# Attention over a graph in one kernel: wider k and q loads by broadcast, two chunks of adj in one load, and a rebuilt head

## Chip, core and metric

The kernel runs on one core of a Trainium2 chip. Its time is the device time of one execution in microseconds (us), given as the median of several runs. One more execution was profiled; the views shown below come from it.

## What is computed

Two layers over a graph of 2708 nodes with 128 features each. Layer 0 is attention with the adjacency matrix added twice to the scores; layer 1 is a two-hop graph convolution. Each adds its input and normalises. Cut to what matters:

```python
# layer 0: x (2708, 128), adj (2708, 2708), 8 values per query ("heads" are the inner dimension)
q = (x @ Wq.T).reshape(128, 2708, 8)        # a reshape of the flat product, not a transpose
k = (x @ Wk.T).reshape(128, 2708, 8)
v = (x @ Wv.T).reshape(128, 2708, 8)
a = einsum('dnh,dmh->dnm', q, k) * 128 ** -0.5 + adj + adj
out = einsum('dnm,dmh->dnh', softmax(a, axis=2), v).reshape(2708, 1024)
x = layernorm(x + out @ Wo.T)
# layer 1
hidden = adj @ (x @ W2) + b2
x = layernorm(x + adj @ (hidden @ W4) + b4 + hidden @ res_w.T + res_b)
```

So 128 separate attentions over 2708 x 2708 scores are to be made, each with an inner dimension of 8. Because q, k and v are reshapes of the flat product, attention d reads rows d x 2708 / 128 and on of the projection: the first four attentions need the first 85 of the 2708 rows of x, and no more.

## The kernel before

**Stages.** There are three. The head projects the first 256 rows of x and loads the first keys. The attention stage runs over 32 groups of GB = 4 attentions, in each over 6 blocks of QB = 452 queries, in each over 9 steps: 1728 steps. The end divides by the sums, applies Wo, and computes layer 1. All engines run an order written out at build time (manual_schedule): each engine's queue holds its instructions in program order, so an instruction that waits holds up all behind it on that engine. Nearly all loads and stores stand on SP's queue.

**A step.** Keys are cut into 22 chunks m: 21 of 128 and a short one of 20 (number NU = 21). Scores of two (chunk, attention) pairs at a time go to PSUM (`score`, L451), DVE adds the adj tile (`add_near`, L458) and writes them to e, ACT takes the exponential of up to eight of them at once (L559). For nine chunks (TWO_EXP) the exponentials of scores and of adj are taken apart: ACT L556 makes w from scores in PSUM, and POOL L557 multiplies w by the exponential of adj (ecol), which is computed once in group 0, stored in DRAM (ne), and loaded in all later groups. PE then adds the products with the values (`add_up`, L468 to L476), and `hand_on` (L479) copies the sums to SBUF and stores them (os). `interleave` fixes the order of PE's work from a table of costs.

**Loads.** `load_adj` (L303) loads one tile of [128, 452] of adj, stored with chunk rows contiguous (adjP): `col` tiles of one chunk, `two` tiles of two chunks (two loads; the short chunk comes from adjS), or an `ecol`. The loop keeps 8 such loads ahead of the step it is at. `load_keys` (L261) brings k of the next group to SBUF (k_raw): 128 partitions, of which 8 at a time get the high or low half of the split k, in 16 loads. Each half stands in two places, since a score is a product of sums: k high and low against q high and low. The loads stand in steps 0, 2, 4 to 30 of the group before. `order_keys` then puts k in order of chunks (9 casts on POOL, L275), `load_values` and `spread_values` do the same for v. `load_q` (L295) loads q of the next block (8 loads of 16 rows, at step 3 of a block).

**Projections.** `project_all` (head) makes 128 rows of K, Q or V at once, splits K and Q into a high and a low part (ACT L402, DVE L403), and returns the store. The rest of the rows are projected by quarters inside the attention loop (`load_quarter`, `project`).

**The head before.** It loads x, the three weights and two adj tiles, projects and stores all 128 rows of K and Q, projects V, loads k (16 loads, on SP and ACT in turn) and q, stores V, loads six adj tiles and the values, then projects rows 128 to 255, and orders the keys:

```python
        for i in range(2):
            project_all(0, i)()
        store_v = project_all(0, 2)
        for h in range(16):
            load_keys(0, h, nc.scalar if h % 2 else nc.sync)
        load_q(0, 0, (nc.sync, nc.scalar))
        store_v()
```

Of the kernel before, what the change touches and what calls it, by code (L numbers as in the profile page):

```python
# [18 lines left out]
P = 128  # L19
H = 8  # L20
GB = 4
NB = 512
QB = 452
# [116 lines left out]


@with_exitstack
def graph_attention_gcn(ctx: ExitStack, tc: tile.TileContext, x, xT, adj, adjT, adjP, adjS,
                        WqT, WkT, WvT, WoT, W2, b2, W4, b4, res_wT, res_b, out):


# [22 lines left out]
    half_scale = 0.5 * D ** -0.5  # L169
# [32 lines left out]
    with ExitStack() as s:  # L202
# [58 lines left out]
        def load_keys(g, h, queue=nc.sync):  # L261


            if h == 0:
                groups[g] = kpool.tile([P, NU, P], F32R, tag="k", name="k"), k_short[g % 2], vals[g % 2], v_short[g % 2]
                raw_keys[g] = raw.tile([P, N], F32R, tag="k_raw", name="k_raw")
            queue.dma_start(raw_keys[g][ds(H * h, H), :].bitcast(F32),
                              ks[ds(H * (h % 4 // 2), H), ds((GB * g + h // 4) * N, N)])

        def order_keys(g, i, copy=nc.gpsimd.tensor_copy):  # L270

            t, (k, kz, _, _) = raw_keys[g], groups[g]
            if i < 8:
                n = P // 8
                copy(k[:, :, ts(i, n)], t[:, ts(i, n * NU)].rearrange("p (q c) -> p c q", c=NU))  # L275
            else:
                for j in range(GB):
                    r = ds(32 * j, 32)
                    copy(kz[r, ds(32 * j, SHORT)], t[r, ds(P * NU, SHORT)])
# [12 lines left out]
            nc.gpsimd.tensor_copy(to[:, j, :, :H], v)  # L292
            nc.gpsimd.tensor_copy(v_first[g % 2][:, ds(32 * j, H)], v[:, first_chunk, :])

        def load_q(g, b, queues=(nc.sync, nc.sync)):  # L295
            n0, nw = QBS[b]
            q = queries[g, b] = qpool.tile([P, QB], F32R, tag="q", name="q")
            for j in range(GB):
                for i in range(2):
                    queues[i].dma_start(q[ds(32 * j + 2 * H * i, 2 * H), :nw].bitcast(F32),  # L300
                                      qs[:, ds((GB * g + j) * N + n0, nw)])

        def load_adj(n):  # L303
            g, b, m = loads[n]
            n0, nw = QBS[b]
            if isinstance(m, tuple):
                t = adj_cols[g, b, m] = twos.tile([P, 2, QB], F32, tag="two", name="two")
                for i, x in enumerate(m):
                    nc.sync.dma_start(t[:, i, :nw], (adjS if x == NU else adjP[ds(x * P, P), :])[:, ds(n0, nw)])
            elif m < 0 and g > 0:  # L310
                t = exp_cols[g, b, -1 - m] = ecols.tile([P, QB], F32, tag="ecol", name="ecol")
                nc.sync.dma_start(t[:, :nw], near_exp[b, -1 - m][:, :nw])
            else:
                t = adj_cols[g, b, m] = cols.tile([P, QB], F32, tag="col", name="col")
                m = -1 - m if m < 0 else m
                nc.sync.dma_start(t[:, :nw], adjP[ds(m * P, P), ds(n0, nw)])

        ahead = 8
        epool = s.enter_context(tc.tile_pool(name="weights", bufs=5))
# [30 lines left out]

        def project(n):
# [27 lines left out]

            return [split, store, load]  # L380

        first_x = flat(ppool.tile([P, 3, QB], F32, tag="w", name="w"))
        nc.sync.dma_start(first_x[:, : FIRST * P], xT[:, : FIRST * P])
        first_w = flat(epool.tile([P, 8, QB], F32, tag="e", name="e"))
        for i, (w, _) in enumerate(projections):
            nc.sync.dma_start(first_w[:, ds(2 * NB * i, 2 * NB)], w)
        for n in range(2):
            load_adj(n)
        load_quarter(0)

        def project_all(c, i):

            dst = projections[i][1]
            pp = ps.tile([P, 2, NB], F32, tag="s", name="s")
            for h in range(2):
                nc.tensor.matmul(pp[:, h, :], first_x[:, ts(c, P)], first_w[:, ts(2 * i + h, NB)], start=True, stop=True)
            o = flat(epool.tile([P, 8, QB], F32, tag="e", name="e"))[:, : 4 * NB].rearrange("p (l f) -> p l f", l=2)
            if i == 2:
                nc.scalar.copy(o[:, 0], flat(pp))
                return lambda: nc.sync.dma_start(dst.rearrange("(i g) e -> i (g e)", g=P)[ts(c, P)], o[:, 0])  # L400
            f = half_scale if i == 1 else 1.0
            nc.scalar.mul(o[:, 0].bitcast(F32R), flat(pp), f)  # L402
            nc.vector.scalar_tensor_tensor(o[:, 1].bitcast(F32R), flat(pp), f, o[:, 0], ALU.mult, ALU.subtract)  # L403
            return lambda: nc.sync.dma_start(dst.rearrange("r (i g) -> i r g", g=P)[ts(c, P)],
                                             o.rearrange("p l (e g) -> p (l e) g", g=P))


        for i in range(2):
            project_all(0, i)()
        store_v = project_all(0, 2)  # L410
        for h in range(16):
            load_keys(0, h, nc.scalar if h % 2 else nc.sync)
        load_q(0, 0, (nc.sync, nc.scalar))
        store_v()
        for n in range(2, ahead):
            load_adj(n)
        for j in range(GB):
            load_values(0, j)
        for i in range(3):
            project_all(1, i)()  # L420
        for h in range(9):
            order_keys(0, h, (nc.gpsimd.tensor_copy, nc.vector.tensor_copy, nc.scalar.copy)[h % 3])
        for j in range(GB):
            spread_values(0, j)

# [53 lines left out]
        def hand_on(g, b):  # L479
            n0, nw = QBS[b]  # L480
            o = opool.tile([P, QB], F32, tag="o", name="o")
            nc.vector.tensor_copy(o[:, :nw], acc.pop((g, b))[:, :nw])  # L482
            queue = nc.gpsimd if (g, b) == (NG - 1, len(QBS) - 1) else nc.sync
            for j in range(GB):
                queue.dma_start(os_[:, ds((GB * g + j) * N + n0, nw)], o[ds(32 * j, H + 1), :nw])

        where = {}

# [2 lines left out]
        for g in range(1, NG):  # L491
            c = (min(NG, g + 2) * GB * N - 1) // (P * P)
            assert c < FIRST or amid[quarters.index((c, 2, 3))] + 8 < 54 * g
        jobs = []
        loaded = ahead
        for what, n, c, beside in interleave(plan, len(steps) // len(plan), NU, amid, bufs=5):
            if what == "amid":
# [5 lines left out]
                add_up(g, b, c, where.pop((g, b, c)))  # L503
                continue
            if what == "hand_on":
                hand_on(*divmod(n, len(QBS)))
                continue
            g, b, i = steps[n]
            pieces, two, _ = plan[i]
            nw = QBS[b][1]  # L510
            if c == 1 and jobs:
                jobs.pop(0)()
            if c == 0:
                nq = (g, b + 1) if b + 1 < len(QBS) else (g + 1, 0)
                if i == 3 and nq[0] < NG:
                    load_q(*nq)

                if g + 1 < NG:
                    t = b * len(plan) + i
                    if t < 32 and t % 2 == 0:  # L520
                        load_keys(g + 1, t // 2)
                    elif t < 32 and t % 8 == 7:
                        load_values(g + 1, t // 8)
                    elif 33 <= t < 50 and t % 2:
                        order_keys(g + 1, (t - 33) // 2)
                    elif t >= 50:
                        spread_values(g + 1, t - 50)
                if g == NG - 1 and i % 2 and early:
                    nc.sync.dma_start(*early.pop(0))
                last = max(loads.index((g, b, x), max(0, loaded - 40)) for x in [chunks_of(p) for p in pieces] + [-1 - two])  # L530
# [567 lines left out]
```

## Time and profile before

| what | value |
|---|---|
| median of 3 runs | 6857.9 us (6836.81 to 6862.31) |
| profiled execution | 6849.71 us, span 6847.9 us |
| granted clock | 0.993 |
| busy share of the span | PE 97%, ACT 95%, DVE 89%, POOL 85% |
| DMA | 1665.68 MB, mean 243 GB/s, q1 79.7% of 16 engines |
| DMA issues on SP: two 1920, q 1532, k 504, col 2358, ecol 1674 | of about 8900 in all |
| k load, q load, adj tile | 84.6 KB, 28.2 KB, 226 KB |

Times are from the start of the span. A line of a group or of the order of time names the line of the kernel, the engine, the operation, and what it writes and reads ("k_raw<-ks"). SPq and ACTq are DMA issues on the queues of SP and ACT. In the list of waits, each line gives who waited for whom, the total in us, the number of times and the longest. A busy PE is not PE at its peak, since matmuls are pipelined; an engine that is idle and not the bottleneck costs nothing.

### The profile page before, as it was taken

Reading aid. Unit: us, or ns where it says so; the run is one execution under the profiler, and the core shown is the slowest. Engines: PE = TensorE matmul, PEld = TensorE weight load, DVE = VectorE, ACT = ScalarE, POOL = GpSimd, SP = SyncE. Lnnn points to the kernel's source line nnn. Section 1 sums busy time; section 2 is a strip of 40 time slices with the busy share of each in tenths; the row PEclk is TensorE's granted clock in tenths of the full one; section 3 lists DMA queues with packets and bytes.
Section 4 is the critical chain, followed back from the end, with each engine's and each line's share of the span. In section 5 each row is a group of like instructions: output and inputs, shape, how many; then the busy total and the mean of one; then the engine's idle time right before and its main releaser. Section 6 shows DMA issues by size and latency. Waiting matters only on the chain.

```text
span 6847.9 us, 138426 instructions
## 1 busy us (share of the span) xinstructions
PE 6633.7 (97%) x50612; PEld 1982.5 (29%) x50612; DVE 6117.5 (89%) x6368; ACT 6504.6 (95%) x3660; POOL 5791.3 (85%) x2710
## 2 busy tenths in 40 slices
PE   7999999999999999999999999999999999999999
PEld 2222222222222222222222222222222222222254
DVE  5899999999999999999999999999999899999962
ACT  7999999999999999999999999999999999999930
POOL 5898988999988999989899989899998888888810
PEclk8999999999999999999999999999999999999999
DMA  8888888888888888888888888888888887777774
GB/s 244 265 248 249 254 251 242 250 245 244 248 248 253 245 250 250 251 245 249 244 245 249 248 253 252 251 241 249 247 245 240 233 242 233 234 234 235 233 262 131
DMA packets 1148664, 1665.68 MB, mean 243 GB/s; under 512 B 151560, under 2 KB 1130804, under 8 KB 1141300
## 3 DMA queue, kind: packets, MB, share of 16 engines
q1 hardware_dynamic: 1144808, 1654.51, 79.7%
q8 instruction: 401, 6.57, 0.4%
q10 hardware_dynamic: 3040, 2.19, 0.1%
q14 instruction: 287, 2.35, 0.1%
q0 software_dynamic: 128, 0.06, 0.0%
HBM read 1574.37 MB, written 81.80 MB: 242 GB/s over the span
## 4 chain that ended last, share of the span: by engine, by line
PE 46%; DMA 16%; DVE 9%; POOL 9%; issue 7%; SPq 7%; ACT 6%; DVEq 0%; POOLq 0%; ACTq 0%
PE acc L476 22%; PE s L451 14%; DVE e L458 8%; POOL w L557 8%; DMA col<-in_adjP 6%; SPq L300 4%; DMA two<-in_adjP 3%; ACT e L559 3%; DMA ecol<-ne 3%; ACT w L556 3%; PE acc L468 2%; PE acc L660 2%; PE acc L742 2%; PE p L451 1%; DMA k_raw<-ks 1%
## 5 line engine op out<-in xcount | busy, mean ns | idle before, releaser
L557 POOL TENSOR_TENSOR w<-w,ecol 128x1356 f32<-128x1356 f32 (+1 forms) x1728 | 5347.0, 3101 | 692.6 <-ACT w L556 615.7
L458 DVE TENSOR_TENSOR e<-s,col 128x904 f32<-128x904 f32 (+1 forms) x4608 | 4817.2, 1092 | 316.4 <-PE s L451 76.0
L559 ACT ACTIVATE e<-e 128x2712 f32<-128x2712 f32 (+5 forms) x1728 | 4635.5, 2683 | 19.3 <-DVE e L458 14.3
L476 PE MATMUL acc<-e,vals 128*9 128x452 f32 x20352 | 3564.0, 546 | 0.0
L451 PE MATMUL s<-q,k 32*128 32x452 f32 x10944 | 2495.0, 461 | 130.2 <-DVE e L458 95.5
L556 ACT ACTIVATE w<-p 128x1356 f32<-128x1356 f32 (+1 forms) x1728 | 2328.6, 1348 | 12.8 <-PE p L451 9.1
L451 PEld LDWEIGHTS s<-q,k 32*128 32x128 f32 x10944 | 1003.9, 182 | 3248.4 <-DVE e L458 2864.9
L476 PE MATMUL acc<-w,vals 128*9 128x452 f32 x10368 | 1627.4, 546 | 0.0
L451 PE MATMUL p<-q,k 32*128 32x452 f32 (+1 forms) x5184 | 1324.9, 445 | 21.8 <-ACT w L556 19.8
L458 DVE TENSOR_TENSOR e<-s,two 128x904 f32<-128x904 f32 (+1 forms) x960 | 1049.0, 1093 | 109.0 <-PE s L451 60.5
L476 PEld LDWEIGHTS acc<-e,vals 128*9 128x9 f32 x20352 | 442.3, 88 | 779.3 <-issue 778.1
L451 PEld LDWEIGHTS p<-q,k 32*128 32x128 f32 x5184 | 546.4, 182 | 50.5 <-ACT w L556 43.1
L476 PEld LDWEIGHTS acc<-w,vals 128*9 128x9 f32 x10368 | 209.9, 88 | 177.4 <-issue 161.0
L275 POOL CAST k<-k_raw 128x336 fp32r<-128x336 f32 x251 | 222.2, 885 | 35.9 <-DMA q<-qs 35.9
L473 PE MATMUL acc<-e,v_first 128*32 128x452 f32 (+1 forms) x1536 | 186.7, 558 | 12.7 <-ACT e L559 0.6
L468 PE MATMUL acc<-e,v_short 128*128 128x452 f32 (+1 forms) x384 | 196.7, 594 | 0.0
L357 PE MATMUL s<-wc,xc 128*128 128x256 f32 (+1 forms) x480 | 166.6, 429 | 4.7
L482 DVE COPY o<-acc 128x452 f32<-128x452 f32 x192 | 120.3, 627 | 46.1 <-PE acc L476 46.1
L359 DVE TENSOR_SCALAR pa<-s 128x256 f32<-128x256 f32 (+1 forms) x240 | 100.4, 418 | 31.6 <-PE s L357 23.7
L373 POOL TENSOR_TENSOR pr<-pa,pr 128x256 fp32r<-128x256 f32 (+1 forms) x160 | 117.5, 735 | 12.8
L357 PEld LDWEIGHTS s<-wc,xc 128*128 128x128 f32 (+1 forms) x480 | 69.6, 183 | 155.6 <-DVE e L458 152.5
L660 PE MATMUL acc<-rows,x 128*128 128x512 f32 (+2 forms) x252 | 105.1, 553 | 0.0
(91 smaller groups left out, 1029.5 us busy)
## 6 DMA issues: line engine op xcount, KB each, us to landing
col<-in_adjP SPq DMA_DIRECT2D x1965, 226.0 KB
two<-in_adjP SPq DMA_DIRECT2D x1440, 226.0 KB
ecol<-ne SPq DMA_DIRECT2D x1395, 226.0 KB
col<-in_adjP SPq DMA_DIRECT2D x393, 224.0 KB
two<-in_adjP SPq DMA_DIRECT2D x288, 224.0 KB
ecol<-ne SPq DMA_DIRECT2D x279, 224.0 KB
k_raw<-ks SPq DMA_DIRECT2D x504, 84.6 KB
two<-in_adjS SPq DMA_DIRECT2D x160, 226.0 KB
```

What stands on the lines that cost most here:

```text
L275: copy(k[:, :, ts(i, n)], t[:, ts(i, n * NU)].rearrange("p (q c) -> p c q", c=NU))
L300: queues[i].dma_start(q[ds(32 * j + 2 * H * i, 2 * H), :nw].bitcast(F32), qs[:, ds((GB * g + j) * N + n0, nw)])
L357: nc.tensor.matmul(pp[:mi, 0, :QW], given[c][:, :mi], given.pop((c, i, h)), start=True, stop=True)
L451: nc.tensor.matmul(to[:, :nw], k[r, m, :], q[r], start=True, stop=True)
L458: nc.vector.tensor_add(e[:, ds(at, 2), :nw], st[:, :, :nw], a)
L468: nc.tensor.matmul(a[:, :nw], vz, e[:, t, :nw], start=False, stop=False)
L473: nc.tensor.matmul(a[ds(32 * j, 32), :nw], v_first[g % 2][:, ds(32 * j, 32)], e[:, t, :nw], start=True, stop=False)
L476: nc.tensor.matmul(a[ds(32 * j, VW), :nw], v[:, m, ds(VW * j, VW)], e[:, t, :nw], start=False, stop=(m == last_chunk))
L556: nc.scalar.activation(w[:, :, :nw], sp[:, :, :nw], AF.Exp, scale=2.0)
L557: nc.gpsimd.tensor_mul(w[:, :, :nw], w[:, :, :nw], exp_cols[g, b, two][:, :nw].unsqueeze(1).to_broadcast([P, 3, nw]))
L559: nc.scalar.activation(e[:, :at, :nw], e[:, :at, :nw], AF.Exp, scale=2.0)
L660: nc.tensor.matmul(accs[k][:, :nw], x1[:mw, m, :], rows[m][:mw, ds(n0, nw)], start=(m == 0), stop=(m == NM - 1))
```

## The change

1. k: 8 loads of 16 partitions in place of 16 of 8. Each reads 8 rows of ks twice, through an access pattern with a leading dimension of 2 and step 0 (`to_broadcast`). In the loop they stand in steps 2, 6, 10 to 30.
2. q: 4 loads of 32 partitions in place of 8 of 16, in the same way, one in each of steps 3 to 6.
3. adj: the short chunk is put in front of adjP, and a `two` tile is one load of [128, 2, 452].
4. The stores of the sums go out one in each step, in place of four at once.
5. The head: WkT comes on ACT's queue; ACT and DVE split K and Q by halves of 512 columns; of K and Q only rows 0 to 84 are stored first (K's high and low part apart), the other 43 later, after the loads of the first eight adj tiles; V's 128 rows are stored whole. The key loads of the high parts come ahead of those of the low parts. Rows 128 to 255 are stored after that, and `load_quarter(0)` comes last.
6. In the head, k is put in order by ranges of three chunks over all partitions, on DVE, ACT and POOL, in place of by 16 key positions.

```diff
             if h == 0:
                 groups[g] = kpool.tile([P, NU, P], F32R, tag="k", name="k"), k_short[g % 2], vals[g % 2], v_short[g % 2]
                 raw_keys[g] = raw.tile([P, N], F32R, tag="k_raw", name="k_raw")
-            queue.dma_start(raw_keys[g][ds(H * h, H), :].bitcast(F32),
-                              ks[ds(H * (h % 4 // 2), H), ds((GB * g + h // 4) * N, N)])
+            part = ks[ds(H * (h % 2), H), ds((GB * g + h // 2) * N, N)]
+            queue.dma_start(raw_keys[g][ds(2 * H * h, 2 * H), :].bitcast(F32), part.unsqueeze(0).to_broadcast([2, H, N]))
...
-        def load_q(g, b, queues=(nc.sync, nc.sync)):
+        def load_q(g, b, j, queue=nc.sync):
             n0, nw = QBS[b]
-            q = queries[g, b] = qpool.tile([P, QB], F32R, tag="q", name="q")
-            for j in range(GB):
-                for i in range(2):
-                    queues[i].dma_start(q[ds(32 * j + 2 * H * i, 2 * H), :nw].bitcast(F32),
-                                      qs[:, ds((GB * g + j) * N + n0, nw)])
+            if j == 0:
+                queries[g, b] = qpool.tile([P, QB], F32R, tag="q", name="q")
+            part = qs[:, ds((GB * g + j) * N + n0, nw)]
+            queue.dma_start(queries[g, b][ds(32 * j, 32), :nw].bitcast(F32), part.unsqueeze(0).to_broadcast([2, 2 * H, nw]))
+
+        chunk_rows = adjP.rearrange("(c p) n -> p c n", p=P)
...
                 t = adj_cols[g, b, m] = twos.tile([P, 2, QB], F32, tag="two", name="two")
-                for i, x in enumerate(m):
-                    nc.sync.dma_start(t[:, i, :nw], (adjS if x == NU else adjP[ds(x * P, P), :])[:, ds(n0, nw)])
+                x, x1 = ((i + 1) % NM for i in m)
+                nc.sync.dma_start(t[:, :, :nw], chunk_rows[:, ds(x, 2, step=x1 - x), ds(n0, nw)])
...
+        first_w = flat(epool.tile([P, 8, QB], F32, tag="e", name="e"))
+        nc.scalar.dma_start(first_w[:, : 2 * NB], WkT)
         first_x = flat(ppool.tile([P, 3, QB], F32, tag="w", name="w"))
         nc.sync.dma_start(first_x[:, : FIRST * P], xT[:, : FIRST * P])
...
+        near_rows = 0, (GB * N - 1) // P + 1
+        far_rows = near_rows[1], P - near_rows[1]
+        whole = 0, P
+        k0 = project_all(0, 0)
+        for l in range(2):
+            put(k0, 0, 0, near_rows, l)
+        q0 = project_all(0, 1)
+        put(q0, 0, 1, near_rows)
+        for l in range(2):
+            for j in range(GB):
+                load_keys(0, 2 * j + l, nc.scalar if j % 2 else nc.sync)
+        v0 = project_all(0, 2)
+        put(v0, 0, 2, whole)
+        for j in range(GB):
+            load_q(0, 0, j)
+        for n in range(2, 5):
             load_adj(n)
         for j in range(GB):
             load_values(0, j)
-        for i in range(3):
-            project_all(1, i)()
-        for h in range(9):
-            order_keys(0, h, (nc.gpsimd.tensor_copy, nc.vector.tensor_copy, nc.scalar.copy)[h % 3])
+        for n in range(5, ahead):
+            load_adj(n)
+        others = [project_all(1, i) for i in range(3)]
+        put(k0, 0, 0, far_rows)
+        put(others[0], 1, 0, whole)
+        put(q0, 0, 1, far_rows)
+        put(others[1], 1, 1, whole)
+        put(others[2], 1, 2, whole)
+        load_quarter(0)
...
+        for c, n, copy in ((0, 3, nc.vector.tensor_copy), (3, 3, nc.scalar.copy), (6, 3, nc.gpsimd.tensor_copy),
+                           (9, 3, nc.vector.tensor_copy), (12, 3, nc.scalar.copy), (15, 3, nc.gpsimd.tensor_copy),
+                           (NU, 0, nc.scalar.copy), (18, 3, nc.gpsimd.tensor_copy)):
+            order_first(c, n, copy)
...
+            if c == 1 and sums:
+                sums.pop(0)()
             if c == 0:
                 nq = (g, b + 1) if b + 1 < len(QBS) else (g + 1, 0)
-                if i == 3 and nq[0] < NG:
-                    load_q(*nq)
+                if 3 <= i < 3 + GB and nq[0] < NG:
+                    load_q(*nq, i - 3)
...
-                    if t < 32 and t % 2 == 0:
-                        load_keys(g + 1, t // 2)
+                    if t < 32 and t % 4 == 2:
+                        load_keys(g + 1, t // 4)
```

The new `put(o, c, i, rows, l)` stores rows r0 to r0 + n of a projected tile (K and Q as rows of 128 values, 512 bytes each, to ks or qs; for K one half at a time where l is given), and `order_first(c, n, copy)` casts chunks c to c + n of k_raw into k over all 128 partitions.

More of the change, by code (lines that the diff above doesn't have):

```diff
@@ L142, in graph_attention_gcn @@
 @with_exitstack
-def graph_attention_gcn(ctx: ExitStack, tc: tile.TileContext, x, xT, adj, adjT, adjP, adjS,
+def graph_attention_gcn(ctx: ExitStack, tc: tile.TileContext, x, xT, adj, adjT, adjP,
                         WqT, WkT, WvT, WoT, W2, b2, W4, b4, res_wT, res_b, out):
@@ L315, in load_adj @@
                 m = -1 - m if m < 0 else m
-                nc.sync.dma_start(t[:, :nw], adjP[ds(m * P, P), ds(n0, nw)])
+                nc.sync.dma_start(t[:, :nw], chunk_rows[:, m + 1, ds(n0, nw)])
         ahead = 8
@@ L380, in project @@
             return [split, store, load]
+        first_w = flat(epool.tile([P, 8, QB], F32, tag="e", name="e"))
+        nc.scalar.dma_start(first_w[:, : 2 * NB], WkT)
         first_x = flat(ppool.tile([P, 3, QB], F32, tag="w", name="w"))
         nc.sync.dma_start(first_x[:, : FIRST * P], xT[:, : FIRST * P])
-        first_w = flat(epool.tile([P, 8, QB], F32, tag="e", name="e"))
-        for i, (w, _) in enumerate(projections):
-            nc.sync.dma_start(first_w[:, ds(2 * NB * i, 2 * NB)], w)
+        for i in range(1, 3):
+            nc.sync.dma_start(first_w[:, ds(2 * NB * i, 2 * NB)], projections[i][0])
@@ L387, in graph_attention_gcn @@
         for n in range(2):
             load_adj(n)
-        load_quarter(0)
         def project_all(c, i):
-            dst = projections[i][1]
             pp = ps.tile([P, 2, NB], F32, tag="s", name="s")
+            f = half_scale if i == 1 else 1.0
+            if i == 2:
+                o = flat(ppool.tile([P, 3, QB], F32, tag="w", name="w"))[:, : 2 * NB].unsqueeze(1)
+            else:
+                o = flat(epool.tile([P, 8, QB], F32, tag="e", name="e"))[:, : 4 * NB].rearrange("p (l f) -> p l f", l=2)
@@ L395, in project_all @@
             for h in range(2):
+                r = ts(h, NB)
                 nc.tensor.matmul(pp[:, h, :], first_x[:, ts(c, P)], first_w[:, ts(2 * i + h, NB)], start=True, stop=True)
-            o = flat(epool.tile([P, 8, QB], F32, tag="e", name="e"))[:, : 4 * NB].rearrange("p (l f) -> p l f", l=2)
-            if i == 2:
-                nc.scalar.copy(o[:, 0], flat(pp))
-                return lambda: nc.sync.dma_start(dst.rearrange("(i g) e -> i (g e)", g=P)[ts(c, P)], o[:, 0])
-            f = half_scale if i == 1 else 1.0
@@ L402, in project_all @@
[L402 to L412, printed above, removed]
@@ L413, in graph_attention_gcn, with put @@
-        load_q(0, 0, (nc.sync, nc.scalar))
-        store_v()
-        for n in range(2, ahead):
+                if i == 2:
+                    nc.scalar.copy(o[:, 0, r], pp[:, h, :])
+                else:
+                    nc.scalar.mul(o[:, 0, r].bitcast(F32R), pp[:, h, :], f)
+                    nc.vector.scalar_tensor_tensor(o[:, 1, r].bitcast(F32R), pp[:, h, :], f, o[:, 0, r], ALU.mult, ALU.subtract)
+            return o
+        def put(o, c, i, rows, l=None):
+            r0, n = rows
+            dst, r = projections[i][1], ds(c * P + r0, n)
+            if i == 2:
+                nc.sync.dma_start(dst.rearrange("(i g) e -> i (g e)", g=P)[r], o[ds(r0, n), 0])
+                return
+            l0, ls = (0, 2) if l is None else (l, 1)
+            nc.sync.dma_start(dst.rearrange("r (i g) -> i r g", g=P)[r, ds(H * l0, H * ls)],
+                              o[ds(r0, n), ds(l0, ls)].rearrange("p l (e g) -> p (l e) g", g=P))
@@ L418, in graph_attention_gcn, with order_first @@
             load_values(0, j)
-        for i in range(3):
-            project_all(1, i)()
-        for h in range(9):
-            order_keys(0, h, (nc.gpsimd.tensor_copy, nc.vector.tensor_copy, nc.scalar.copy)[h % 3])
+        for n in range(5, ahead):
[7 more added lines that the diff above has]
+        load_quarter(0)
+        def order_first(c, n, copy):
+            t, (k, kz, _, _) = raw_keys[0], groups[0]
+            if n:
+                copy(k[:, ds(c, n), :], t[:, : P * NU].rearrange("p (q c) -> p c q", c=NU)[:, ds(c, n), :])
+            else:
+                order_keys(0, 8, copy)
+        for c, n, copy in ((0, 3, nc.vector.tensor_copy), (3, 3, nc.scalar.copy), (6, 3, nc.gpsimd.tensor_copy),
+                           (9, 3, nc.vector.tensor_copy), (12, 3, nc.scalar.copy), (15, 3, nc.gpsimd.tensor_copy),
+                           (NU, 0, nc.scalar.copy), (18, 3, nc.gpsimd.tensor_copy)):
+            order_first(c, n, copy)
         for j in range(GB):
@@ L482, in hand_on, with store @@
             nc.vector.tensor_copy(o[:, :nw], acc.pop((g, b))[:, :nw])
-            queue = nc.gpsimd if (g, b) == (NG - 1, len(QBS) - 1) else nc.sync
-            for j in range(GB):
-                queue.dma_start(os_[:, ds((GB * g + j) * N + n0, nw)], o[ds(32 * j, H + 1), :nw])
+            last = (g, b) == (NG - 1, len(QBS) - 1)
+            def store(j):
+                (nc.gpsimd if last else nc.sync).dma_start(os_[:, ds((GB * g + j) * N + n0, nw)], o[ds(32 * j, H + 1), :nw])
+            stores = [lambda j=j: store(j) for j in range(GB)]
+            while last and stores:
+                stores.pop(0)()
+            return stores
         where = {}
@@ L493, in graph_attention_gcn @@
             assert c < FIRST or amid[quarters.index((c, 2, 3))] + 8 < 54 * g
-        jobs = []
+        jobs, sums = [], []
         loaded = ahead
@@ L505, in graph_attention_gcn @@
             if what == "hand_on":
-                hand_on(*divmod(n, len(QBS)))
+                sums += hand_on(*divmod(n, len(QBS)))
                 continue
@@ L1073 @@
         "adjT": adj.T,
-        "adjP": adj.T[: n // P * P].reshape(P, n // P, n).transpose(1, 0, 2).reshape(n // P * P, n),
-        "adjS": adj_short,
+        "adjP": np.concatenate([adj_short, adj.T[: n // P * P].reshape(P, n // P, n).transpose(1, 0, 2).reshape(-1, n)]),
         "WqT": by_head(L0_gnn_Wq),
```

## The prediction

> **What bounds the kernel now.** I read the busy time of each engine by stretches first, then the waits of ACT, then the DMA share by stretches inside one group, then the head in order of time. In the stretches, the columns are the length, the busy time of PE, PEld, DVE, ACT and POOL (with counts), the granted clock, the mean busy share of the 16 DMA engines, and GB/s.
>
> ```profile
> core 0: us, PE busy (x) PEld busy (x) DVE busy (x) ACT busy (x) POOL busy (x), PEclk, DMA share, GB/s
> 46.00:500.00 454.00, 425.36 (x3150) 121.74 (x3149) 390.07 (x390) 443.29 (x332) 375.84 (x187) 0.96 0.86 262
> 500.00:1500.00 1000.00, 980.39 (x7677) 280.41 (x7675) 926.74 (x938) 996.14 (x537) 900.23 (x425) 1.00 0.83 249
> ...
> 4500.00:5500.00 1000.00, 977.72 (x7628) 279.40 (x7624) 922.04 (x932) 989.79 (x533) 893.54 (x421) 0.99 0.82 246
> ...
> 1250.00:1260.00 10.00, 10.00 (x78) 2.84 (x74) 9.02 (x10) 10.00 (x6) 9.98 (x5) 1.00 1.03 379
> 1288.00:1408.00 120.00, 117.67 (x924) 33.65 (x924) 111.82 (x114) 119.44 (x65) 104.40 (x43) 1.00 0.85 245
> 1408.00:1489.00 81.00, 79.38 (x628) 22.62 (x624) 74.66 (x77) 80.94 (x45) 75.99 (x41) 1.00 0.77 248
> ```
>
> ACT is the bound of the attention stage: in 500 to 1500 us it is busy 996 of 1000. Its two exponentials come 537 times per 1000 us, so a step (two of them) takes 3.72 us; a block of 9 steps 33.5 us, a group of 54 steps 201 us. All of ACT's idle time between 46 and 6500 us is about 37 us, and it waits for operands, hardly for a queue:
>
> ```profile
> ACT e L559 <- DVE e L458: 14.3, 32, 0.9
> ACT w L556 <- PE p L451: 9.1, 8, 3.6
> ...
> ACT ecol L431 <- DMA col<-in_adjP: 5.1, 4, 3.2
> ```
>
> SP's waits are larger, but they are paid ahead of time:
>
> ```profile
> SPq L485 <- DVE o L482: 438.6, 166, 8.8
> ...
> SPq L309 <- DMA two<-in_adjP: 134.8, 393, 1.8
> ```
>
> So what the steady part can win is bounded by 37 us (0.5%). It is the DMA that can lose: its engines are 85% busy in the 120 us of a group in which the next group's keys come in, 77% in the other 81 us.
>
> The head, in order of time (start, duration):
>
> ```profile
> 10.73 0.40 SPq L404 DMA_DIRECT2D ks<-e  x1
> ...
> 12.50 0.54 SPq L404 DMA_DIRECT2D qs<-e  x1
> ...
> 15.96 15.10 SPq L267 DMA_DIRECT2D k_raw<-ks  x8
> 15.97 14.32 ACTq L267 DMA_DIRECT2D k_raw<-ks  x8
> ...
> 35.70 5.19 SPq L300 DMA_DIRECT2D q<-qs  x4
> ...
> 45.75 1.09 PE L451 MATMUL s<-q,k 32*128 32x452 f32 x4 [2.73 <-DMA two<-in_adjP]
> ```
>
> ```profile
> 21.00:31.00 10.00, 0.00 (x0) 0.00 (x0) 0.00 (x0) 0.00 (x0) 0.00 (x0) 0.50 0.50 70
> ```
>
> In 21 to 31 us the loads of k are all that moves. The share is 0.50: a load whose outermost size is 8 rows keeps eight of sixteen engines busy and no more.
>
> **What the change does to that.** The row says: 8 rows, 8 engines. The Trainium skill, "DMA: Bandwidth & Descriptors", section "Why a DMA increments its semaphore by 16 and not by 1" (how many engines), generalises it: a DMA runs on the largest k up to 16 that divides the slowest non-1 size of both access patterns, on SP and ACT the lowest-numbered k engines; its "Rules for kernel authors" say that a leading zero-stride broadcast of c copies confines a DMA to c engines. The share of 0.50 agrees; no run here shows 2, 5 or 1. This rule speaks against the change. The new k and q loads read `part.unsqueeze(0).to_broadcast([2, ...])`, so their outermost size is 2, and the rule puts all of both on engines 0 and 1. The new 85-row stores would run on 5 engines and the 43-row ones on one. By the row alone (a load keeps the spread it has today) the change is worth the small gain of the third case below; by the rule, this sum:
>
> *Work of engine 0 in the 120 us of key loading in one group.*
> - All loads and stores other than k and q. 245 GB/s over 120 us are 29.4 MB; less k (16 x 84.6 KB = 1.4 MB) and q (3.6 blocks x 8 x 28.2 KB = 0.8 MB), 27.2 MB, 1.70 MB per engine. Unhindered an engine moves 379/16/1.03 = 23.0 GB/s (the row at 1250): 74 us, the lower end. Today's share gives 0.85 x 120 = 102, less some 8 us of k and q: 94 us, the upper end. I take 80, near the lower end: in the trace's packet records 1,808-byte rows take a median of 75 ns, and 131 ns on average where they overlap a row of k, 89 elsewhere; what hinders them today is mostly k and q.
> - k: 8 loads of 16 rows, half on engine 0: 64 rows of 10,832 bytes. In the packet records such a row takes 0.41 us unhindered, 0.61 on average, 0.54 to 0.57 with one or two in flight: 26, 39, and taken 35 us.
> - q: 3.6 blocks x 4 loads x 16 rows = 230 rows of 1,808 bytes at 0.079 (23.0 GB/s) to 0.13 us: 18 to 30, taken 23.
>
> Sum 138 us (118 to 163) where 120 are to be had. The excess of 18 us is cushioned once per group by the lead of 8 adj loads, 2.1 steps or 8 us, which the quiet 81 us refill (80 x 81/120 = 54 of other work and 157 rows of q, 16 us: 70 of 81). Left: 10 us in each of 31 groups, **+310 us** (0 at the lower end; 35 x 31, about +1,100, at the upper). What is late then is an adj or ecol tile, so DVE's L458 and POOL's L557 wait, ACT behind them, and SP waits for landings with everything in its queue behind it.
>
> *Head.* Today the first scores run at 45.75 us. A 512-byte packet takes 27 ns in the packet records. After, on engine 0, from a first store at about 9 us (ACT and DVE work by halves, and WkT comes on ACT's queue): K's near rows twice 680 packets over 5 engines, 3.7 us each; Q's near rows 1,360 packets, 7.3 us; k 64 rows at 0.41, 26 us; q 64 rows at 0.08, 5 us; three adj loads 2 us. That is 48 us, first scores near 57: +11. Then the far rows of K and Q, 43 x 16 = 688 packets each on one engine, 18.6 us each, stand on SP ahead of the ninth adj load: 37 us, of which 8 are covered by the eight tiles in hand: +29. Together **+40** (+20 where these overlap the stalls of today's head, ACT idle 9 of the 80 us after 46; +60 if they add to them; below zero only if the loads spread).
>
> *Edits I cost at nothing.* One load instead of two for the two-chunk tiles saves 960 issues of about 0.43 us on SP, same bytes, 128 rows outermost and so 16 engines as now; q saves 768 issues and k 256; q's and the sums' stores are spread over steps where today 4 stores and 8 loads stand in a clump (1.4 and 3.6 to 4.1 us of SP). All of it is hidden by the prefetch and by ACT; if that cover is gone it is worth part of the 37 us of idle ACT, 0 to -15, and where engines 0 and 1 set the pace it is worth nothing. Moved in the head: load_quarter(0), from before the stores to behind the far ones; its first use is at step 8, five steps behind the stalled tiles. Key ordering by chunk ranges is the same 21 x 128 casts on three engines as today (L275), with the first chunks earlier: 0 to -2.
>
> **Sum.** Profiled execution 6849.7 us (span 6847.9 and 1.8 around it) + 310 + 40 = 7199.7; it lies 8.2 below the median of the three runs (6857.9), so 7208 for the median. A measurement of this kernel can tell about 0.5% (34 us) from no change.
>
> **Rivals.**
> 1. *Narrow, and saturated* (likeliest, chance 0.66): 7208. Its own range is 6930 to 7600: an excess of 10 to 30 us a group, less the lead of 8, in 31 groups, with a head of +20 to +60.
> 2. *Narrow, but two engines keep up* (0.16): with rows at their unhindered times engine 0 needs 118 of 120 us, so no group is slower and only the head costs: 6858 + 20 to 60, 6878 to 6918. For it: the median row takes 75 ns. Against: 98% leaves no room for bunched loads, and every landing counts all engines it uses.
> 3. *The loads still spread, and the change wins* (0.18). One mechanism: if a broadcast load were put on 8 or 16 engines, the head's k, 20 us at 70 GB/s on half the engines, would take about half (-10), the first stores -3, shorter clumps on SP another -5 to -15 of the 37: about 6835, 6815 to 6850. It decides from the point where a k load keeps 8 engines or more. For it: SP's and DMA's waits in the chain are then shorter. Against: the 0.50 above shows that the outermost size decides.
>
> That the change doesn't do what it says is case 1 itself: the loads are larger in bytes and narrower in engines.
>
> **Numbers.** Slower by over 0.5% (above 6892): all of case 1 and 0.11 of case 2, 0.77. Within 0.5%: 0.05 of case 2 and 0.09 of case 3, 0.14. Faster: the other 0.09 of case 3. The range reaches from 6850, the upper end of case 3, to 7520; below it lies most of case 3, above it case 1 with an excess of more than about 27 us a group.
>
> **What would show it.** Right: in the head, a stretch with k loads alone has a DMA share near 0.13 (2 of 16), not 0.50; first scores near 57 us; a gap of some 30 us in ACT before 110 us, while the far rows go out at a share near 0.06; in a group's key-loading part ACT is under 95% busy with the mean DMA share below today's 0.85, and in the quiet part near 99%; L458 and L557 wait for col, two and ecol. Wrong: a share of 0.5 or more in the head's k loads; ACT still 99.6% busy in 500 to 1500 us (then 2 or 3); a loss as large in quiet parts as in key-loading parts (then it is not engines 0 and 1 but the SP queue or the larger tiles).

## The result, and the profile after

The changed kernel takes 7051.02 us (median of 4 runs, 7041.83 to 7053.68) where the kernel before, run beside it, took 6850.28 (median of 4 runs, 6836.81 to 6862.31): a ratio of 1.0296 (95% interval 1.028 to 1.0312), slower by some 203 us. The profiled execution has a span of 7051.9 us. Line numbers below are those of each kernel's own file; the exponentials L556, L557 and L559 of before are L603, L604 and L606 after, the adj addition L458 is L497, the scores L451 are L490.

The stretches of the changed kernel (same columns as before: length, busy PE, PEld, DVE, ACT, POOL, granted clock, DMA share, GB/s):

```profile
46.00:500.00 454.00, 373.55 (x2649) 105.95 (x2652) 330.93 (x331) 382.19 (x302) 314.98 (x149) 0.87 0.76 233
500.00:1500.00 1000.00, 961.96 (x7464) 273.35 (x7456) 900.63 (x911) 971.30 (x521) 875.90 (x417) 0.99 0.78 240
...
3240.00:3370.00 130.00, 124.85 (x968) 35.34 (x970) 116.69 (x119) 125.73 (x68) 113.38 (x51) 0.99 0.78 238
...
3450.00:3580.00 130.00, 122.76 (x948) 34.53 (x944) 113.56 (x116) 122.35 (x67) 107.57 (x43) 0.97 0.73 218
3580.00:3660.00 80.00, 78.49 (x613) 22.68 (x609) 74.08 (x76) 79.94 (x44) 76.48 (x47) 1.00 0.84 267
```

ACT is busy 971 of 1000 us where it was 996. The last two rows split a group: in the 130 us in which keys come in ACT has 94%, in the quiet 80 us 99.9%. In the key part of the group before (from 3240) it has 96.7%; over the 24 groups between 500 and 5500 us the trace gives a mean of 95.6% (each from the first issue of a k load to 12 us behind the last), with 10 of them under 95%. The mean DMA share in the key part at 3450 is 0.73, below the 0.85 of before: the transfers are late while most engines have nothing to do. ACT's three longest waits for operands in the stage come to 186 us, where they were 29:

```profile
ACT w L603 <- PE p L490: 104.1, 88, 4.3
...
ACT e L606 <- DVE e L497: 54.3, 56, 16.3
...
ACT ecol L470 <- DMA col<-in_adjP: 28.0, 7, 17.1
```

SP's waits, which before named adj tiles and the sums, now name the keys, behind a wait for the projections (POOL's pr) that was there before as well:

```profile
SPq L378 <- POOL pr L373: 330.8, 76, 7.1
SPq L313 <- DMA k_raw<-ks: 286.7, 83, 4.8
SPq L310 <- DMA k_raw<-ks: 219.2, 56, 5.8
```

The head in order of time (start, duration), and two stretches of it, one with k loads alone, one with a far store alone:

```profile
11.31 2.24 SPq L418 DMA_DIRECT2D ks<-e  x2
...
17.50 4.48 ACTq L268 DMA_DIRECT2D k_raw<-ks  x4
18.04 21.20 SPq L268 DMA_DIRECT2D k_raw<-ks  x4
...
56.44 0.71 PE L490 MATMUL s<-q,k 32*128 32x452 f32 x1 [21.41 <-DMA q<-qs]
...
63.77 15.57 SPq L418 DMA_DIRECT2D ks<-e  x2
79.39 19.35 SPq L418 DMA_DIRECT2D qs<-e  x2
```

```profile
30.00:35.00 5.00, 3.08 (x6) 0.97 (x6) 1.72 (x3) 1.65 (x3) 0.00 (x0) 1.00 0.13 55
70.00:75.00 5.00, 0.00 (x0) 0.00 (x0) 0.00 (x0) 0.00 (x0) 1.71 (x1) 0.50 0.07 22
```

0.13 is two engines of sixteen, 0.07 one. The first scores run at 56.4 us (45.75 before). ACT's busy time in the first 150 us is 57.94 us where it was 103.75: the head costs 46 us. Of these, 33 are two gaps, of 16.26 us up to 84.86 and of 17.09 us up to 109.96, behind the far stores. The other 157 us or so, by subtraction, are lost in the steps after it.

### The profile page after: what moved, and what is told of

Same layout as the page of the kernel before. It is cut to its first block, busy times and chain, and to the rows that moved or that the text cites. A ratio compares the mean times of both kernels' runs of the same rounds, so it can differ in the third digit from the quotient of the medians.

```text
span 7051.9 us, 135857 instructions
## 1 busy us (share of the span) xinstructions
PE 6696.7 (95%) x50612; PEld 1987.3 (28%) x50612; DVE 6118.1 (87%) x6371; ACT 6524.6 (93%) x3666; POOL 5790.5 (82%) x2710
## 4 chain that ended last, share of the span: by engine, by line
PE 46%; DMA 26%; DVE 11%; ACT 6%; issue 6%; SPq 3%; POOL 2%; DVEq 0%; ACTq 0%; POOLq 0%
PE acc L515 23%; PE s L490 14%; DVE e L497 10%; DMA col<-in_adjP 8%; DMA two<-in_adjP 5%; DMA ecol<-ne 4%; DMA q<-qs 4%; ACT w L603 3%; ACT e L606 3%; POOL w L604 2%; PE acc L507 2%; PE p L490 1%; PE acc L707 1%; PE acc L789 1%; DMA k_raw<-ks 1%
## 5 line engine op out<-in xcount | busy, mean ns | idle before, releaser
L604 POOL TENSOR_TENSOR w<-w,ecol 128x1356 f32<-128x1356 f32 (+1 forms) x1728 | 5345.8, 3100 | 886.4 <-ACT w L603 788.0
L497 DVE TENSOR_TENSOR e<-s,col 128x904 f32<-128x904 f32 (+1 forms) x4608 | 4813.7, 1091 | 442.2 <-PE s L490 124.4
L606 ACT ACTIVATE e<-e 128x2712 f32<-128x2712 f32 (+5 forms) x1728 | 4631.9, 2681 | 61.4 <-DVE e L497 54.3
L490 PE MATMUL s<-q,k 32*128 32x452 f32 x10944 | 2506.1, 465 | 243.7 <-DVE e L497 189.8
L603 ACT ACTIVATE w<-p 128x1356 f32<-128x1356 f32 (+1 forms) x1728 | 2324.6, 1345 | 125.2 <-PE p L490 104.1
L490 PEld LDWEIGHTS s<-q,k 32*128 32x128 f32 x10944 | 1006.7, 183 | 3403.7 <-DVE e L497 2973.4
L515 PE MATMUL acc<-w,vals 128*9 128x452 f32 x10368 | 1647.0, 551 | 0.0
L490 PE MATMUL p<-q,k 32*128 32x452 f32 (+1 forms) x5184 | 1337.1, 447 | 19.1 <-ACT w L603 17.8
L497 DVE TENSOR_TENSOR e<-s,two 128x904 f32<-128x904 f32 (+1 forms) x960 | 1047.8, 1092 | 118.2 <-PE s L490 52.5
L490 PEld LDWEIGHTS p<-q,k 32*128 32x128 f32 x5184 | 551.0, 184 | 43.7 <-ACT w L603 37.5
```

Source lines behind the costliest of these rows:

```text
L490: nc.tensor.matmul(to[:, :nw], k[r, m, :], q[r], start=True, stop=True)
L497: nc.vector.tensor_add(e[:, ds(at, 2), :nw], st[:, :, :nw], a)
L515: nc.tensor.matmul(a[ds(32 * j, VW), :nw], v[:, m, ds(VW * j, VW)], e[:, t, :nw], start=False, stop=(m == last_chunk))
L603: nc.scalar.activation(w[:, :, :nw], sp[:, :, :nw], AF.Exp, scale=2.0)
L604: nc.gpsimd.tensor_mul(w[:, :, :nw], w[:, :, :nw], exp_cols[g, b, two][:, :nw].unsqueeze(1).to_broadcast([P, 3, nw]))
L606: nc.scalar.activation(e[:, :at, :nw], e[:, :at, :nw], AF.Exp, scale=2.0)
```

## The experiments

All ratios are against the kernel before, run on the same chip. For all kernels at once: the ratio, ACT's busy time in the 5000 us from 500 to 5500, its busy time in the first 150 us, and the sum of SP's waits that name k_raw in 500 to 5500 us (with the number of waits).

| kernel | ratio (95% interval) | ACT, 500 to 5500 | ACT, 0 to 150 | SP for k_raw |
|---|---|---|---|---|
| before | 1 | 4977 | 104 | 99 (197) |
| changed | 1.0296 (1.028 to 1.0312) | 4860 | 58 | 706 (180) |
| e1 wide k and q | 1.0009 (1.0003 to 1.0016) | 4993 | 84 | 43 (58) |
| e2 k in 8 rows | 1.0023 (1.0012 to 1.0033) | 4992 | 77 | 70 (153) |
| e3 q in 16 rows | 1.0243 (1.0226 to 1.026) | 4902 | 62 | 699 (180) |
| e4 96 rows first | 1.0243 (1.0224 to 1.0263) | 4869 | 86 | 698 (180) |
| e5 wide, 96 rows | 0.9966 (0.9954 to 0.9978) | 4993 | 111 | 48 (66) |
| e6 before, narrow k and q | 1.077 (1.0754 to 1.0787) | 4585 | 98 | 694 (171) |
| e7 e3, k in half columns | 1.0117 (1.0099 to 1.0135) | 4967 | 62 | 573 (358) |
| e8 stores on POOL | 1.017 (1.0154 to 1.0186) | 4938 | 58 | 686 (171) |
| e9 q at once | 1.0572 (1.0555 to 1.059) | 4720 | 57 | 664 (173) |
| e10 two loads | 1.0413 (1.0395 to 1.043) | 4804 | 58 | 713 (179) |
| e11 sums at once | 1.0489 (1.0471 to 1.0508) | 4765 | 58 | 672 (177) |
| e12 before, narrow k | 1.0772 (1.0754 to 1.079) | 4588 | 97 | 728 (170) |

**Which dimension is outermost (e1).** The number of loads and the bytes written are the same; the order of the dimensions differs. A q load puts the row outside and its copy inside. A k load is no longer a broadcast: it reads the high and the low half of each of 8 rows, in place of one half of 8 rows twice, and the second copy comes with the next load.

```diff
-            part = ks[ds(H * (h % 2), H), ds((GB * g + h // 2) * N, N)]
-            queue.dma_start(raw_keys[g][ds(2 * H * h, 2 * H), :].bitcast(F32), part.unsqueeze(0).to_broadcast([2, H, N]))
+            part = ks.rearrange("(l r) n -> r l n", l=2)[:, :, ds((GB * g + h // 2) * N, N)]
+            queue.dma_start(raw_keys[g][ds(2 * H * h, 2 * H), :].bitcast(F32), part)
...
-            queue.dma_start(queries[g, b][ds(32 * j, 32), :nw].bitcast(F32), part.unsqueeze(0).to_broadcast([2, 2 * H, nw]))
+            queue.dma_start(queries[g, b][ds(32 * j, 32), :nw].bitcast(F32), part.unsqueeze(1).to_broadcast([2 * H, 2, nw]))
```

Expected: 

> The changed kernel with the same number of k and q loads and the same bytes, but the dimensions in another order: row outermost and copy inside it, so that the outermost size is 8 for k and 16 for q (the rows of k and q stand in another order in SBUF, the same in both). Two-engine theory: the steady loss goes. ACT is 99.5% busy or more in 500 to 1500 us (97.1% in the changed kernel), a stretch of the head with k loads alone has a share of about 0.50 in place of 0.13, and the time falls by some 140 us of steady loss and 0 to 20 of the head, to 6890 to 6920 us. Rival, that the larger tiles or fuller queue of SP cost the time: nothing of this changes, 7030 to 7070 us.

Measured: 1.0009, 6850.87 us. A stretch of the head with k loads on both queues beside the last of q's store, and then ACT's share in the stage:

```profile
25.00:30.00 5.00, 3.76 (x4) 1.17 (x4) 0.00 (x0) 1.17 (x2) 0.00 (x0) 0.50 0.52 167
...
500.00:1500.00 1000.00, 983.79 (x7702) 282.63 (x7698) 928.58 (x941) 998.66 (x539) 903.09 (x423) 1.00 0.81 249
```

The share is 0.52: eight engines (by the rule of the prediction the store's five are among them; the share cannot tell). ACT has 99.9%, better than before the change. The larger tiles and the fuller queue cost nothing. The gain of 197 us is larger than I expected, since the head gains as well: in this stretch 65 of the packets are rows of k, 0.70 MB in 5 us or 140 GB/s, where loads of 8 rows moved 70 before; so the first exponential of w starts at 44.24 us (60.91 changed, 48.57 before).

**k or q (e2, e3).** Each load of one of them is split in two as before the change; first e2, then e3.

```diff
+            for i in range(2):
+                queue.dma_start(raw_keys[g][ds(2 * H * h + H * i, H), :].bitcast(F32),
+                                ks[ds(H * (h % 2), H), ds((GB * g + h // 2) * N, N)])
```

```diff
+            for i in range(2):
+                queue.dma_start(queries[g, b][ds(32 * j + 2 * H * i, 2 * H), :nw].bitcast(F32), part)
```

Expected of e2: 

> The changed kernel with each k load split into two loads of 8 rows (as before the change: 16 loads per group, no broadcast); q stays a broadcast on two engines. Theory of saturation: engine 0 has 80 + 10 + 23 = 113 of 120 us to do while keys come in, so nearly all of the steady loss goes: 6900 to 6930 us, ACT over 99% in 500 to 1500 us. Rival, that each narrow load delays the tiles behind it however much room there is: only k's part of the loss goes, some 60% of it, 6950 to 6990 us.

Expected of e3: 

> The changed kernel with each q load split into two of 16 rows (as before the change: 8 loads per block on 16 engines); k stays a broadcast on two engines. Theory of saturation: engine 0 has 80 + 26 to 35 + 3 = 109 to 118 of 120 us to do, so most of the steady loss goes: 6910 to 6960 us. Rival, that each narrow load delays the tiles behind it however much room there is: q's part alone goes, some 40% of it, 6980 to 7010 us.

Measured: e2 1.0023, e3 1.0243. k in 8 rows frees the steady part completely, though q is still on two engines; with some 19 us of ACT in the head it is below both expectations. With q wide and k narrow, ACT still misses 76 us of its 4977 (the changed kernel misses 117). My saturation theory is wrong there: engine 0 has at most 118 of 120 us to do in e3, and yet two thirds of the loss stay. e3 lies in the range of its rival, but the same rival missed e2 by 90 us. e2 issues as many k loads as the kernel before and loses nothing in the steady part, so narrow q alone costs nothing; with k narrow as well, q adds some 36 us. It is k that must be explained.

**The rows stored first (e4).**

```diff
-        near_rows = 0, (GB * N - 1) // P + 1
+        near_rows = 0, 96
```

Expected: 

> The changed kernel with 96 rows of K and Q stored first and 32 later, in place of 85 and 43: both divide by 16. Two-engine theory extended to the stores (5 engines for 85 rows, one for 43): the head's stall behind the far rows goes and the first stores land some 10 us earlier on the loaded engines: 35 to 50 us less, 7000 to 7015 us, and no stretch with a DMA share near 0.07. Rival, that the head's loss is due to k and q alone: 0 to 15 us less, 7035 to 7050 us.

Measured: 1.0243, 36 us less by the ratios, 46 by the medians. ACT gains 28 us in the first 150 us, the first exponential of w starts at 54.72 in place of 60.91, and the stretches of 0.07 are gone. That fits the extended theory; the one engine for 43 rows is seen in the share, the five for 85 are only argued.

**Both repairs (e5).** Both diffs above.

Expected: 

> Both repairs on the changed kernel: k and q with row outermost (8 and 16 engines, as in the first experiment), and 96 rows stored first and 32 later (16 engines). If the two costs are separate, the 40 us or so that the far rows still cost in the first experiment's head go: 6800 to 6820 us, 0.4 to 0.7% faster than the kernel before, with over 100 us of ACT busy time in the first 150 us. If the head's stall only moves to the next transfer: 6835 to 6850 us.

Measured: 0.9966 (0.9954 to 0.9978), 6823.12 us, faster than both kernels by a little; the interval excludes no change. By the ratio to e1 it gains 29 us rather than 40, so the upper end of my expectation was missed. ACT waits for DVE and PE under 2 us in all between 500 and 5500.

**The loads alone on the kernel before (e6, e12).** The loop's k loads (e12), or k and q (e6), are the changed kernel's broadcasts; all else is the kernel before.

```diff
+            elif h % 2:
+                part = ks[ds(H * (h % 4 // 2), H), ds((GB * g + h // 4) * N, N)]
+                queue.dma_start(raw_keys[g][ds(H * (h - 1), 2 * H), :].bitcast(F32), part.unsqueeze(0).to_broadcast([2, H, N]))
...
+                if (g, b) != (0, 0):
+                    queues[0].dma_start(q[ds(32 * j, 32), :nw].bitcast(F32), part.unsqueeze(0).to_broadcast([2, 2 * H, nw]))
+                    continue
```

Expected of e6: 

> The kernel before with one part of the change alone: k and q in the loop are loaded by the changed kernel's broadcast (outermost size 2); the head, the two-chunk tiles and the stores stay as they were. Two-engine theory: the whole steady loss and none of the head's, 130 to 160 us more than before: 6975 to 7010 us. Rival, that it takes the two-chunk loads or the spread stores as well: 6850 to 6920 us.

Expected of e12: 

> The kernel before with the loop's k loads alone as broadcasts of outermost size 2; q as before, 8 loads of 16 rows. If k's long landing is what costs, as the second and third experiment say: 300 to 450 us more than before, 7150 to 7300 us. If it is q's clump of four narrow loads: 6900 to 7000 us.

Measured: 1.077 (7376.86 us) and 1.0772 (7365.68 us). Both expectations of e6 missed, and e12 lies above its own: the same narrow loads cost over three times as much on the kernel before as in the changed one. e12 shows that nearly all of it is k. So the edits I had costed at nothing, which the kernel before lacks, save some 370 us once k is narrow.

**Half the burst (e7).** On e3: each k load in two loads of half the columns, two steps apart.

```diff
+            c0, cw = (0, 1354) if part_of == 0 else (1354, N - 1354)
...
-                    if t < 32 and t % 4 == 2:
-                        load_keys(g + 1, t // 4)
+                    if t < 32 and t % 2 == 0:
+                        load_keys(g + 1, t // 4, part_of=t // 2 % 2)
```

Expected: 

> The kernel of the third experiment (changed kernel, q in loads of 16 rows) with each k load cut into two loads of half the columns, two steps apart: the same two engines, the same work on them per group, half the burst and half the time to landing. Saturation of engine 0 (work in the phase against time in the phase): the loss stays, 6995 to 7015 us. Theory of the burst, that the load's long landing uses up the lead of the tiles and of the eight transfers SP has in flight: about half of the steady 90 us goes, 6950 to 6975 us, and SP's waits for k_raw fall by half or more.

Measured: 1.0117, 6921.51 us, less than either theory said; ACT misses 11 us where e3 missed 76. Engine 0 has the same work, so saturation, as a sum over 120 us, falls; half the load also lands sooner (by the kept trace a median of 5.7 us after issue, 7.8 in e3). SP still waits for keys 573 us in all, not half: but 358 times for 1.6 us, in place of 180 times for 3.9. Many short waits cost little, few long ones much.

```profile
SPq L323 <- DMA k_raw<-ks: 141.1, 86, 2.9
```

**SP's other waits (e8).** The stores of the projected quarters in the loop are issued by `nc.gpsimd` in place of `nc.sync`.

```diff
-                return [lambda: nc.sync.dma_start(to, a), load]
+                return [lambda: nc.gpsimd.dma_start(to, a), load]
```

Expected: 

> The changed kernel with the stores of the projected quarters in the loop (ks, qs, vs from pr and pa) issued on POOL's queue in place of SP's, so that SP no longer waits for POOL and DVE there (315 and 134 us in 500 to 5500 us). k and q stay on two engines. Theory that SP's stalls use up the lead and the two engines only keep it from coming back: over half of the steady loss goes, 6930 to 6975 us. Saturation alone: no gain, 7040 to 7060 us. POOL pays for 380 more issues and is 82% busy; if that is dear the time rises in both.

Measured: 1.017, 86 us less by the ratios; ACT misses 39 us in place of 117. SP's waits for k are the same. So more than half of the steady loss comes where the projections and the narrow k meet on SP's queue. Taking these stores away removes SP's stops for POOL and DVE there, but also frees places among its eight; this run does not part the two. A natural control points the same way: in 5500 to 6400 us, where the projections are done, the changed kernel's ACT is busy 895 of 900 us with the same narrow k. The projections are hit themselves, too: in 500 to 5500 us PE, which runs in program order, waits 30 us for their weights, in e8 4, and in the kernel before it shows no such wait:

```profile
PE s L358 <- DMA wc<-in_WkT: 18.3, 8, 3.6
PE s L358 <- DMA wc<-in_WqT: 11.8, 12, 1.6
```

**The edits costed at nothing, one undone at a time (e9, e10, e11, in this order).**

```diff
+                if i == 3 and nq[0] < NG:
+                    for j in range(GB):
+                        load_q(*nq, j)
...
+                for i, xi in enumerate((x, x1)):
+                    nc.sync.dma_start(t[:, i, :nw], chunk_rows[:, xi, ds(n0, nw)])
...
-            while last and stores:
+            while stores:
```

Expected of e9: 

> The changed kernel with its four q loads of a block issued together at step 3 again (one per step in the changed kernel). The kernel before with narrow k and q alone lost 529 us, the changed kernel some 155 in its steady part, so one of the edits that I had costed at nothing pays for about 380. Window theory (eight transfers in flight, the eighth after a k load waits for its landing 8 to 10 us later): the clump puts four short transfers of the window in one place, 7070 to 7150 us. Burst on engine 0 (four times 16 rows at once): 7200 us or more.

Expected of e10: 

> The changed kernel with the two-chunk tiles loaded by two transfers of 226 KB again, in place of one of 452 KB; the same bytes. Window theory: the seven transfers that may follow a k load before SP has to wait for it carry fewer tiles, so most of the 380 us come back: 7250 to 7400 us. Two-engine saturation: the bytes on engine 0 are the same, 7040 to 7070 us.

Expected of e11: 

> The changed kernel with the four stores of the sums issued together when a block ends (one per step in the changed kernel). Window theory: four more places of the window used at once, and SP waits for the copy of the sums with all its loads behind it: 7060 to 7120 us. If the stores' place does not matter: 7040 to 7060 us.

Measured: 1.0572, 1.0413 and 1.0489, so undoing one costs 189, 80 and 132 us. Together 401, about what parts e6 (7.7%) from the changed kernel's steady loss (2.3%): 370 us; they were not undone together. My window theory had the sign, and all three results miss its ranges: the two loads cost much less than it said, the clumps of q and of the sums more. e9, at 7234.59 us, lies where the rival was expected, a burst of q on engine 0 (7200 or more), and that is not excluded. Against it stands that the kernel before, with narrow k, loses the same with q's clump in four narrow loads (e6) and in eight wide ones (e12).

## Why the prediction was right, and where it was not

**Right.** The direction, and its ground: a load's outermost size sets its engines. The share of 0.13 in the head's k loads was forecast and came, and one engine for the far rows; e1 and e4 show the ground, as other sizes outermost take most of the loss away. The head was forecast at +40 and cost 46, with the first scores at 56.4 (57 forecast); ACT falls to 94% in one key part, 95.6% on average, and stays at 99.9% in the quiet one shown (forecast under 95 and near 99), with a DMA share below 0.85. That the time lies in the forecast's range is in part luck: the range was wide, and the steady part's +310 came from a sum that does not hold, as follows.

**Mis-sized.** The steady part was forecast at +310 and cost some 157. The term of k took 0.55 us for a row on engine 0. In the stretch from 30 to 35 us two engines move 55 GB/s, so a row takes 10,832 bytes / 27.5 GB/s = 0.39 us, near the 0.41 that the prediction had for a row unhindered. With other packets about, the packet records overlap (a mean share of 1.03 in the prediction's own row at 1250 says so) and don't add. That makes 25 us of the 35. With it the sum is 128, and less the lead of 8 it says no loss at all. The lead is mis-sized as well: a block takes 26 tiles in its 9 steps (12 col, 5 two, 9 ecol), so 8 tiles are 2.8 steps or 10 us, where the prediction has 2.1 steps and 8 us.

**The step that failed** is the sum itself: the work of an engine in 120 us against 120 us. e3 (at most 118 with 80 us for all other transfers, or 122 with the upper 94 and k at 25, yet 76 us of ACT lost) and e7 (the same work, 11 lost) refute it. What the runs show in its place can be read off SP's issues of the changed kernel:

```profile
3294.29 0.61 SPq L268 DMA_DIRECT2D k_raw<-ks  x1
3295.01 0.35 SPq L313 DMA_DIRECT2D ecol<-ne  x1
3295.45 0.37 SPq L317 DMA_DIRECT2D col<-in_adjP  x1
3296.09 0.38 SPq L310 DMA_DIRECT2D two<-in_adjP  x1
3296.68 0.95 SPq L378 DMA_DIRECT2D qs<-pr  x2
3297.68 1.26 SPq L525 DMA_DIRECT2D os<-o  x1
3298.99 0.63 SPq L300 DMA_DIRECT2D q<-qs  x1
3302.80 0.36 SPq L286 DMA_DIRECT2D v_raw<-vs  x1
```

After a k load come seven transfers, then SP stands still until the k load has landed, 8.5 us after its issue. In e6 the same holds at another place: k at 3056.72, seven issues, the next at 3066.65. So eight transfers are in flight at most, and one that lands late stops the queue. The cap is a wait in the program: in the kept trace SP's transfers raise eight semaphores in turn, and the one at 3302.80 waits for the semaphore that the k load raises. It was not varied.

The stop is not the only delay. The tiles issued behind a narrow k load land late themselves: over 500 to 5500 us of the changed kernel a col tile lands a median of 8.8 us after its issue where a k load is in flight, and 4.5 us where none is (5.0 and 4.3 in the kernel before). Followed back through the profile's releasers, a little over half of ACT's idle time there ends at a transfer that was issued with a k load in flight. How much the stop adds to this late landing was not measured apart.

SP's waits for k are about 700 us, 4 us a wait, in every kernel whose narrow k loads are whole, while the loss goes from 1.7 to 7.7%. So the delay by itself does not set the loss. What differs, as I read it, is how much of the lead is left when it comes: the clumps of q (e9) and sums (e11), the doubled loads (e10) and the stops for POOL (e8) all take from the same eight tiles and eight places. That they do so by this way was not measured.

**Costed at nothing, wrongly.** The prediction said that merged and spread transfers are worth nothing where engines 0 and 1 set the pace. There they are worth some 370 to 400 us. Where k is wide they are worth little: e1 gains 16 us of ACT in the 5000 us over the kernel before.

**The rivals.** "Two engines keep up" named the right throughput and the wrong price, as it had no term for landing. "The loads still spread" was refuted by the 0.13; with the k and q loads spread alone, e1 takes 6851, at the upper end of its range (6815 to 6850); e5, with the stores spread as well, takes 6823.

## What to carry to other kernels

Read the outermost size of both access patterns of every load. Here a broadcast of two copies in front confined it to two engines (share 0.13). With the row outermost, the copy inside it for q and both halves of a row in one load for k, the same bytes came in without the loss, at no cost. Sum up each engine, but price a slow transfer by its landing as well: where the program allows a fixed number in flight it delays what is behind it, and whether that reaches the bound seems to depend on the lead the rest of the queue has left. A stall that is hidden today is no free room: the next edit that delays the queue can bring it back.

## What the runs showed of the hardware

A store of 43 rows ran on one engine (share 0.07, 22 GB/s). Loads of k in 16 rows, two to an engine, moved 140 GB/s in the head where loads of 8 rows, one to an engine, moved 70, both on eight engines by the share (0.52 and 0.50); I had not expected that, and why was not tried. A col tile on its way with a narrow k load landed after 8.8 us, without one after 4.5 (medians). The mean granted clock fell with the loss, from 0.993 to 0.98 in the changed kernel and 0.952 in e6, with 0.50 in stretches where PE had nothing to do; how much of the time that adds stays open. It is not to be ruled out, as 96 of the 134 us for which ACT waits in 500 to 5500 us of the changed kernel are waits for PE's scores.
